# Layer 0: block transposes on VectorE from quarter loads, and the bias table split in its compact form

## The chip, the cores and the metric

The kernel runs on one core of a Trainium2 chip. Time is device time in microseconds (us) of one execution; the time of a kernel is the median of several runs. The engines are called PE (TensorE matmul), PEld (its weight loads), DVE (VectorE), ACT (ScalarE), POOL (GpSimd) and SP (SyncE, which here only issues DMAs).

## What is computed

Four layers follow each other on x of shape (4, 8, 512, 512), axes t, b, n, d: each adds to x a function of the group-normalised x. Only layer 0 is touched by the change. It is a block of spiking attention over four time steps t:

```python
def lif(x):                      # over t
    v = v + (xt - v) / 2; spk = v >= 1; v = v * (1 - spk)
q = heads(lif(bn(x @ Wq.T)));  k = heads(lif(bn(x @ Wk.T)));  v = heads(lif(bn(x @ Wv.T)))
scores = einsum('tbhnd,tbhmd->tbhnm', q, k) * scale + bias_table[rel]     # rel = m - n + N - 1
out = lif(einsum('tbhnm,tbhmd->tbhnd', scores, v))
out = out * gate_scale + gate_shift
x = x + lif(bn(out @ Wp.T))
```

There is no softmax, so q (k^T v) and (bias) v are taken apart. H is 8 heads of 64. The input of layer 0 is normalised over groups of two batch entries b for each t. Layer 1 is a 13x13 depthwise convolution, layer 2 a quantised 3x3 convolution, layer 3 a 3x3 convolution.

## The kernel before, in words

Layer 0 works in 32 steps (b, t), t innermost, the state h of each neuron kept in SBUF from one t to the next. A software pipeline handles in iteration n: attention of step n (`attend`), its output projection (`project_out`) interleaved with the input projections of step n+1 (`project_in` for v, k and q in this order, four column groups c each), and the transposes for step n+2.

- **Loads.** `load_x` (line 408) issues four DMAs of 256 KB on SP, one for each 128 rows n: the x of step n+2 (name x), the residual of step n (xr) and the x whose statistics the next group of batch entries needs (xs). All come from one pool, x0, of 10 tiles.
- **Statistics.** `count` (line 414) runs bn_stats on each tile; `group_stats` (lines 175 to 195) turns them into the mean and the reciprocal deviation of a group: small DVE operations, two PE matmuls (line 178) and a power on POOL (line 195).
- **Transposes.** The projections contract over d, so x has to have d on the partitions. `transposed` (lines 460 to 468) lets PE transpose four 128x128 blocks against an identity into a PSUM bank ps_xT (two banks), and DVE evicts it with the normalisation (line 468) to a tile xn. Four xn tiles make a step, six are in the pool. `transpose` is called for k = 0, 1 during the q projection and for k = 2, 3 after it.
- **Projections.** `project_in` (line 485) multiplies in f32 (two PE passes for each of four blocks k) into a PSUM bank ps_in of the pool ps_mm, two banks. For v and k DVE forms the potential (line 450), the spikes (line 490) and what is kept (line 457), and POOL adds a constant row (line 458). For q, which stays transposed, DVE forms potential (443, or 441 at t = 0), spikes (427) and rest (429), and ACT the half (433). At t = 3 nothing is kept.
- **Attention.** `attend` multiplies k by v (ps_kv, line 501), masks the result to kvb (DVE, line 506), and for each pair of heads j multiplies kvb by q (ps_a, line 513, one bank) and v by the bias (ps_b, line 521, two banks). The bias is a Toeplitz matrix, held as three bf16 parts, toep[0..2], each 128 x 8 x 896; DVE forms the spikes so from both (lines 533, 536, 427, 429).
- **Output.** `project_out` (line 548) multiplies so by the projection's weights in two parts into ps_mm, DVE adds spikes to the residual (559) and takes statistics of the sum (563), POOL mirrors the edges (570) and stores (575).

Before the first step the weights are prepared. `load_weights` loads a matrix with row c*128 + p on partition p. `along_free` (lines 331, 332) lays a per-column scale along the free dimension: four times a DVE product of the identity with a column, and a matmul of ones with it. `prepare_in` multiplies v's and k's weights by this scale (line 344). `prepare_bias` (lines 356 to 364) loads for each head the table as a 128x896 Hankel matrix in f32 and splits it in three parts: three ACT casts, one subtraction on DVE and one on POOL. `prepare_out` prepares the output weights.

The order of the instructions on each engine is fixed when the program is built, from their order in the code, a scheduler's own estimate of when operands are ready, and pool sizes. `issue_after(op)` keeps what is traced in its block behind op on op's engine only; it is no wait for other engines. A DMA issued on SP or ACT that waits for a buffer or a completion counter keeps all later ones of that queue waiting.

Of the kernel before, what the change touches and what calls it, by code (L numbers as in the profile page):

```python
# [30 lines left out]
F32 = mybir.dt.float32  # L34
# [9 lines left out]
T, B, N, D, H = 4, 8, 512, 512, 8  # L44
DH = D // H
NC = N // P
G = 4
PAIR = B // G
EPS = 1e-5
# [215 lines left out]
def layer0(  # L265
# [2 lines left out]
    nc = tc.nc  # L268
    half_scale = 0.5 / math.sqrt(D)

    ps_mm = s.enter_context(tc.tile_pool(name="ps_mm", bufs=2, space=PSUM))
    ps_b = s.enter_context(tc.tile_pool(name="ps_b", bufs=2, space=PSUM))
    ps_1 = s.enter_context(tc.tile_pool(name="ps_1", bufs=1, space=PSUM))
    wpool = s.enter_context(tc.tile_pool(name="w0", bufs=1))
# [16 lines left out]
    a_half = wpool.tile([P, 4, NC], F32, name="a_half")  # L291
    c_half = wpool.tile([P, 4, NC], F32, name="c_half")

    xp = s.enter_context(tc.tile_pool(name="x0", bufs=10))
    small0 = s.enter_context(tc.tile_pool(name="s0", bufs=4))
    x1p = s.enter_context(tc.tile_pool(name="x1p", bufs=2))
    state = s.enter_context(tc.tile_pool(name="state", bufs=1))
# [1 line left out]


    def load_weights(n, engine):
        engine.dma_start(wT[n], i[f"wT_{n}"].rearrange("(c p) e -> p c e", p=P))

    nc.scalar.dma_start(cols.rearrange("p a b -> p (a b)"), i["cols"])
    bn = cols[:, :16, :].rearrange("p (n s) c -> p n s c", s=4)
    ones = wpool.tile([P, P], F32, name="ones")
    nc.vector.memset(ones, 1.0)

    def batch_norms():

        neg_half = wpool.tile([P, 4, NC], F32, name="nh0")
        nc.vector.memset(neg_half, -0.5)
        nc.vector.tensor_scalar_add(a_half, bn[:, :, 3, :], EPS)
        nc.gpsimd.tensor_tensor(a_half, a_half, neg_half, op=ALU.pow)
        nc.vector.tensor_mul(a_half, a_half, bn[:, :, 0, :])
        nc.vector.tensor_scalar_mul(a_half, a_half, 0.5)
        c = c_half[:, :3, :]
        nc.vector.scalar_tensor_tensor(
            c, bn[:, :3, 2, :], -1.0, a_half[:, :3, :], op0=ALU.mult, op1=ALU.mult
        )  # L320
        nc.vector.scalar_tensor_tensor(
            c, bn[:, :3, 1, :], 0.5, c, op0=ALU.mult, op1=ALU.add
        )

    def along_free(cols):


        ps = ps_mm.tile([P, D], F32, tag="mm", name="ps_free")
        for c in range(NC):
            diag = work.tile([P, P], F32, tag="diag", name="diag", bufs=2)  # L330
            nc.vector.tensor_scalar_mul(diag, ident, cols[:, c : c + 1])
            nc.tensor.matmul(
                ps[:, c * P : (c + 1) * P], lhsT=ones, rhs=diag, start=True, stop=True
            )
        return ps

# [2 lines left out]

    def prepare_in(n):  # L340
        j = "qkvp".index(n)
        scale = along_free(a_half[:, j, :])
        for k in range(NC):
            nc.vector.tensor_mul(wT[n][:, k, :], wT[n][:, k, :], scale)  # L344
        return nc.scalar.mul(c_twice[n], along_free(c_half[:, j, :]), 2.0).ins

    def prepare_bias():


        n_u = toep[0].shape[2]  # L350
        table = i["table"]
        hankel = state.tile([P, 2, n_u], F32, tag="h_o", name="hankel")
        rest = state.tile([P, 2, n_u], F32, tag="h_p", name="rest")
        for h in range(H):
            src, r = hankel[:, h % 2, :], rest[:, h % 2, :]
            nc.scalar.dma_start(
                src, bass.AP(table.tensor, h * (2 * N - 1), [[1, P], [1, n_u]])
            )
            dst = [w[:, h, :] for w in toep]
            nc.scalar.copy(dst[0], src[:, ::-1])  # L360
            nc.vector.tensor_sub(r, src[:, ::-1], dst[0])
            nc.scalar.copy(dst[1], r)
            nc.gpsimd.tensor_sub(r, r, dst[1])
            nc.scalar.copy(dst[2], r)

    def load_out():
        wp32 = work.tile([P, NC, D], F32, tag="so", name="wp32")
# [3 lines left out]
    def prepare_out(wp32):  # L371
        gate_scale, gate_shift = cols[:, 16, :], cols[:, 17, :]

        shift = ps_1.tile([P, NC], F32, tag="misc", name="shift")
        for e in range(NC):
            for k in range(NC):
                nc.tensor.matmul(
                    shift[:, e : e + 1],
                    lhsT=wp32[:, k, e * P : (e + 1) * P],
                    rhs=gate_shift[:, k : k + 1],  # L380
                    start=k == 0,
                    stop=k == NC - 1,
                )
        c = c_half[:, 3, :]
        nc.vector.tensor_sub(c, shift, bn[:, 3, 2, :])
        nc.vector.tensor_mul(c, c, a_half[:, 3, :])
        nc.vector.scalar_tensor_tensor(c, bn[:, 3, 1, :], 0.5, c, op0=ALU.mult, op1=ALU.add)

        nc.scalar.mul(
            c_twice["p"].rearrange("p (g v) -> p g v", g=PH), phases(along_free(c)), 2.0  # L390
        )
        scale = work.tile([P, D], F32, tag="v", name="scale_p", bufs=3)
        nc.scalar.copy(scale, along_free(a_half[:, 3, :]))
        for k in range(NC):
            wp = work.tile([P, D], F32, tag="v", name="wp_k", bufs=3)
            nc.vector.scalar_tensor_tensor(
                wp.rearrange("p (g v) -> p g v", g=PH), phases(wp32[:, k, :]),
                gate_scale[:, k : k + 1], phases(scale), op0=ALU.mult, op1=ALU.mult,
            )
            nc.scalar.copy(wpT[0][:, k, :], wp)  # L400
            nc.vector.tensor_sub(wp, wp, wpT[0][:, k, :].bitcast(F32))
            nc.scalar.copy(wpT[1][:, k, :], wp)

    def load_x(b, t, name):
        got = []
        for c in range(NC):
            xt = xp.tile([P, D], F32, tag="x", name=f"{name}_{b}_{t}_{c}")
            nc.sync.dma_start(xt, x_in[t, b, c * P : (c + 1) * P, :])
            got.append(xt)
        return got  # L410

    def count(xt, stats, pair):
        for c in range(NC):
# [43 lines left out]
            nc.vector.scalar_tensor_tensor(h, v, 1.0, v, op0=ALU.is_lt, op1=ALU.mult)  # L457
            nc.gpsimd.tensor_add(h, h, c_twice[n])  # L458

    def transposed(xt, k, m, r):  # L460

        ps = ps_1.tile([P, N], F32, tag="xT", name="ps_xT", bufs=2)
        for c in range(NC):
            nc.tensor.transpose(
                ps[:, c * P : (c + 1) * P], xt[c][:, k * P : (k + 1) * P], ident
            )
        xk = work.tile([P, N], F32, tag="xn", name="xn", bufs=6)
        nc.vector.tensor_scalar(xk, ps, m, r, op0=ALU.subtract, op1=ALU.mult)
        return xk

    def new_spikes():
# [126 lines left out]
    def transpose(n, k):  # L598
        if n <= last:
            b, t = steps[n]  # L600
            xns.setdefault(n, []).append(transposed(xs[n], k, *norms[b // PAIR, t]))
            if k == NC - 1:
                del xs[n]

    def load(n):
        if n <= last:
            xs[n] = load_x(*steps[n], "x")

    def next_group(n):
        g, j = divmod(n + 1, PAIR * T)  # L610
# [12 lines left out]
        return band, eye, x, bt  # L623

    load(0)
    load_weights("v", nc.sync)
    statistics(0, 0, 0, xs[0])
    statistics(0, 0, 1, load_x(1, 0, "xs"))
    batch_norms()
    for k in range(NC):  # L630
        transpose(0, k)
    with tc.issue_after(prepare_in("v")):
# [4 lines left out]
    for n in range(-1, last + 1):  # L637
# [7 lines left out]
        if n + 1 <= last:  # L645
            spikes = new_spikes()
            g, j = divmod(n + 1, PAIR * T)
            if n >= 0:
                load(n + 2)
            if j == 2 and g > 0:  # L650
                norm1(g - 1, ps_1)
            if g == 0 and n >= 0 and n + 2 < T:
                statistics(0, n + 2, 0, xs[n + 2])
                statistics(0, n + 2, 1, load_x(1, n + 2, "xs"))
            if n >= 0:
                next_group(n)
        for a, name in enumerate("vkq"):
            for c in range(NC):
                if n + 1 <= last:
                    did = project_in(name, c, xns[n + 1], spikes, steps[n + 1][1])  # L660
                if (n, name, c) == (-1, "v", 0):
                    first += [prepare_in("k"), did, potentials[0]]
                    with ExitStack() as behind:
                        for op in first:
                            behind.enter_context(tc.issue_after(op))
                        load(1)
                        statistics(0, 1, 0, xs[1])
                        statistics(0, 1, 1, load_x(1, 1, "xs"))
                if n >= 0 and a < 2 and c % 2:
                    project_out(so, 2 * a + c // 2, residual[2 * a + c // 2], b, t)  # L670
                if a == 2 and c % 2:
                    transpose(n + 2, c // 2)
# [4 lines left out]
        if n < 0:  # L677
            with ExitStack() as behind:
                for op in first:
                    behind.enter_context(tc.issue_after(op))  # L680
                prepare_bias()
                prepare_out(load_out())
                next_group(n)
                bands1(tc, i, band1d, w_sum, eye, ps_mm, state)
            for name in "op":
                h_of[name] = state.tile([P, NC, N], F32, tag=f"h_{name}", name=f"h_{name}")
# [593 lines left out]
```

## Time and profile before

| what | value |
|---|---|
| median of 3 runs | 2997.45 us (2994.02 to 2998.33) |
| profiled execution, its time | 2993.4 us |
| its span from first to last instruction | 2991.6 us |
| mean granted PE clock | 0.988 |
| PE busy | 2900.4 us (97%) |
| DVE busy | 2243.8 us (75%) |
| POOL, ACT busy | 1035.6 us (35%), 550.0 us (18%) |
| first matmul of the v projection (line 485) | 21.05 us |
| ps_kv of step 0, 1, 31 | 88.59, 166.39, 2089.56 us |
| DMA in a settled step | 67 to 68 GB/s, 22% of the queues' time |

The page cuts the span into 40 slices of 75 us and gives each engine's busy share in tenths. Matmuls are pipelined, so the duration of one (592 ns for a projection pass) is longer than the distance between two (430 ns); a PE that shows as busy can still lose a little between groups. Layer 0 takes the first 28 slices. A window's busy time is that of all its instructions on an engine, overlaps counted once.

### The profile page before, as it was taken

Reading aid. Unit: us, or ns where it says so; the run is one execution under the profiler, and the core shown is the slowest. Engines: PE = TensorE matmul, PEld = TensorE weight load, DVE = VectorE, ACT = ScalarE, POOL = GpSimd, SP = SyncE. Lnnn points to the kernel's source line nnn. Section 1 sums busy time; section 2 is a strip of 40 time slices with the busy share of each in tenths; the row PEclk is TensorE's granted clock in tenths of the full one; section 3 lists DMA queues with packets and bytes.
Section 4 is the critical chain, followed back from the end, with each engine's and each line's share of the span. In section 5 each row is a group of like instructions: output and inputs, shape, how many; then the busy total and the mean of one; then the engine's idle time right before and its main releaser. Section 6 shows DMA issues by size and latency. Waiting matters only on the chain. (4 is left out here: it accounts for less than half of the span.)

```text
span 2991.6 us, 37579 instructions
## 1 busy us (share of the span) xinstructions
PE 2900.4 (97%) x13343; PEld 1391.5 (47%) x13377; DVE 2243.8 (75%) x3883; ACT 550.0 (18%) x859; POOL 1035.6 (35%) x1928
## 2 busy tenths in 40 slices
PE   7999999999999999999999999999999999689999
PEld 3545555555555555555555555555333333223334
DVE  7887788788769868967986886786665566888880
ACT  2200010011010001001000100100111121676674
POOL 3332233333224333323432333341211112676650
PEclk9999999999999999999999999999999999889999
DMA  5312222222222221212221111111877778698865
GB/s 189 109 58 65 78 65 65 65 64 65 78 65 65 65 72 58 78 65 65 65 69 47 58 43 51 51 56 45 208 203 216 204 210 227 160 198 223 220 175 147
DMA packets 274651, 322.16 MB, mean 108 GB/s; under 512 B 21495, under 2 KB 171711, under 8 KB 274351
## 3 DMA queue, kind: packets, MB, share of 16 engines
q1 hardware_dynamic: 212304, 236.70, 29.3%
q0 software_dynamic: 20192, 56.83, 6.1%
q10 hardware_dynamic: 41967, 26.23, 3.0%
q8 instruction: 105, 1.72, 0.3%
q14 instruction: 83, 0.68, 0.1%
HBM read 210.57 MB, written 103.60 MB: 105 GB/s over the span
## 5 line engine op out<-in xcount | busy, mean ns | idle before, releaser
L485 PE MATMUL ps_in<-w_v,xn 128*128 128x512 f32 x1024 | 465.0, 603 | 2.6 <-DVE w_kq L344 2.6
L485 PE MATMUL ps_in<-xn,w_kq 128*128 128x512 f32 x1024 | 452.9, 595 | 5.1 <-DVE v_q L441 3.7
L485 PE MATMUL ps_in<-w_kq,xn 128*128 128x512 f32 x1024 | 449.8, 592 | 0.7 <-DVE v_k L450 0.7
L797 PE MATMUL ps_conv<-x,bt 112*64 112x512 f32 x2048 | 445.1, 592 | 0.1
L521 PE MATMUL ps_b<-toep,vtok 128*64 128x512 bf16 x3072 | 373.6, 383 | 0.0
L433 ACT ACTIVATE h_q<-v_q,c_half 128x512 f32<-128x512 f32 x96 | 69.3, 722 | 1550.6 <-DVE v_q L429 1164.1
L570 POOL COPY x1s<-x1s 128x2 f32<-128x2 f32 (+1 forms) x1024 | 227.4, 276 | 297.8 <-DVE x1s L559 297.8
L548 PE MATMUL ps_out<-wp,so 128*128 128x512 f32 x1024 | 308.5, 443 | 0.0
L458 POOL TENSOR_TENSOR h_v<-h_v,c_v 128x512 f32<-128x512 f32 x96 | 123.2, 1283 | 517.1 <-DVE h_v L457 505.4
L485 PEld LDWEIGHTS ps_in<-xn,w_kq 128*128 128x128 f32 x1024 | 191.9, 190 | 228.1 <-issue 212.4
L485 PEld LDWEIGHTS ps_in<-w_kq,xn 128*128 128x128 f32 x1024 | 194.2, 190 | 222.0 <-issue 205.2
L485 PEld LDWEIGHTS ps_in<-w_v,xn 128*128 128x128 f32 x1024 | 191.6, 192 | 216.9 <-issue 211.5
L797 PEld LDWEIGHTS ps_conv<-x,bt 112*64 112x64 f32 x2048 | 146.1, 135 | 288.4 <-issue 286.7
L521 PEld LDWEIGHTS <-vtok 128*64 128x64 bf16 x3072 | 207.6, 111 | 126.2 <-issue 4.9
L1182 PE MATMUL ps_conv<-x,band_t 64*64 64x512 f32 x2040 | 246.4, 599 | 3.1 <-DVE band_t L1151 3.1
L1047 POOL COPY u<-x 128x512 f32<-128x512 f32 (+1 forms) x172 | 208.7, 1247 | 95.8 <-issue 48.5
L548 PEld LDWEIGHTS ps_out<-wp,so 128*128 128x128 f32 x1024 | 192.5, 188 | 94.6 <-issue 57.8
L559 DVE SCALAR_TENSOR_TENSOR x1s<-v_p,xr 128x256 f32<-128x256 f32 x256 | 187.0, 770 | 14.9 <-DMA x<-x1s 3.9
L195 POOL TENSOR_TENSOR grstd_x<-grstd_x,neg_half 128x1 f32<-128x1 f32 (+1 forms) x28 | 20.9, 748 | 474.0 <-DVE grstd_x L194 474.0
L815 POOL DMA_DIRECT2D x<-xo x128 | 71.4, 565 | 312.5 <-ACT xo L804 298.2
L804 ACT ACTIVATE xo<-ps_conv,off 128x512 f32<-128x512 f32 x128 | 87.7, 687 | 430.6 <-PE ps_conv L797 316.0
L458 POOL TENSOR_TENSOR h_k<-h_k,c_k 128x512 f32<-128x512 f32 x96 | 122.8, 1279 | 116.4 <-DVE h_k L457 116.4
(191 smaller groups left out, 3557.8 us busy)
## 6 DMA issues: line engine op xcount, KB each, us to landing
x<-x SPq DMA_DIRECT2D x64, 917.0 KB
x<-x SPq DMA_DIRECT2D x168, 256.0 KB
x<-x1s POOLq DMA_DIRECT2D x128, 262.0 KB, 2.5
x<-in_x SPq DMA_DIRECT2D x128, 256.0 KB
xr<-in_x SPq DMA_DIRECT2D x128, 256.0 KB
out<-o SPq DMA_DIRECT2D x164, 192.0 KB
xs<-in_x SPq DMA_DIRECT2D x112, 256.0 KB
x<-xo ACTq DMA_DIRECT2D x128, 128.0 KB
```

The costliest lines, as they stand in the source:

```text
L433: nc.scalar.activation(h, v, AF.Identity, bias=c_col, scale=0.5)
L458: nc.gpsimd.tensor_add(h, h, c_twice[n])
L485: mm = nc.tensor.matmul(ps, lhsT=lhsT, rhs=rhs, start=k == 0, stop=k == NC - 1)
L521: nc.tensor.matmul(pb[two * DH : (two + 1) * DH, :], lhsT=v[:, c, h * DH : (h + 1) * DH], rhs=toep[z][:, h, u : u + N], start=c == 0 and z ...
L548: nc.tensor.matmul(ps, lhsT=so[:, k, c * P : (c + 1) * P], rhs=wpT[z][:, k, :], start=k == 0 and z == 0, stop=k == NC - 1 and z == 1,)
L559: nc.vector.scalar_tensor_tensor(own, v.rearrange("p (g v) -> p g v", g=PH)[:, two, :], 1.0, by_phase[:, two, :], op0=ALU.is_ge, op1=ALU.add,)
L570: nc.gpsimd.tensor_copy(x1[:, f, u : u + n], x1[:, fm, um - n + 1 : um + 1][:, ::-1])
L797: mm = nc.tensor.matmul(ps[q * M1 : (q + 1) * M1, :], lhsT=bt[:, z, :], rhs=xt[:, w0 : w0 + N_PS1, z : z + NV], start=z == 0, stop=z == SH ...
L804: nc.scalar.activation(xo[:, a, :], ps, AF.Identity, bias=off[:, t : t + 1])
L815: engine.dma_start(bass.AP(dst.tensor, dst.offset + (q * n_half * W1_OUT * B + b) * D + f * NV, [[B * D, W1_OUT], [W1_OUT * B * D, n_half] ...
L1047: nc.gpsimd.tensor_copy(u[:n_p, j, :].rearrange("p (v g) -> p v g", g=PH), x[:, j, :].rearrange("p (g v) -> p v g", g=PH),)
L1182: mm = nc.tensor.matmul(ps[j][b * HALF : (b + 1) * HALF, :], lhsT=band[half, b, dx, :], rhs=x3[half, s0 + j, dx : dx + D], start=dx == 0, ...
```

## The change

It replaces PE's transposes in layer 0 by DVE's. A DVE transpose exchanges rows and columns within each 32x32 block only; so x is loaded in four quarters, each on 32 partitions: partition 32 q + s holds, for the rows n = 32 j + s, the 128 columns from 128 q on, in runs of 512 bytes. One DVE transpose of 128 x 512 then gives xn for k: partition 32 q + a holds column 128 q + 32 k + a. The weights' rows are loaded in the same order. The normalisation runs in place on the loaded tile, before the transposes. The quarter tile (128 x 2048) has a pool of its own with one buffer; the pool x0 shrinks to 6 tiles; ps_mm takes the two freed PSUM banks.

The bias table is split while compact, on 24 partitions of 341 entries; the three bf16 parts are stored to DRAM in 16 copies of each head and loaded from there as Toeplitz tiles, 24 loads of 16 partitions each on ACT's queue. The scales are transposed to rows once, and `along_free` selects a row by a matmul with a column of the identity, broadcast, as weights. At the start, v's weights follow the statistics' tiles on SP.

```diff
-    ps_mm = s.enter_context(tc.tile_pool(name="ps_mm", bufs=2, space=PSUM))
+    ps_mm = s.enter_context(tc.tile_pool(name="ps_mm", bufs=4, space=PSUM))
...
-    xp = s.enter_context(tc.tile_pool(name="x0", bufs=10))
+    xp = s.enter_context(tc.tile_pool(name="x0", bufs=6))
+    xqp = s.enter_context(tc.tile_pool(name="xq0", bufs=1))
...
     def load_weights(n, engine):
-        engine.dma_start(wT[n], i[f"wT_{n}"].rearrange("(c p) e -> p c e", p=P))
+        rows = i[f"wT_{n}"].rearrange("(q c a) e -> q a c e", c=NC, a=SQ)
+        for q in range(P // SQ):
+            engine.dma_start(wT[n][q * SQ : (q + 1) * SQ], rows[q])
...
+    def as_rows_of(cols):
+        n = cols.shape[1]
+        ps = ps_mm.tile([n, P], F32, tag="mm", name="ps_rows")
+        nc.tensor.transpose(ps, cols, ident)
+        rows = wpool.tile([4 * NC, P], F32, tag="rows", name="rows", bufs=2)
+        nc.scalar.copy(rows[:n], ps)
+        return rows[:n]
...
         for c in range(NC):
-            diag = work.tile([P, P], F32, tag="diag", name="diag", bufs=2)
-            nc.vector.tensor_scalar_mul(diag, ident, cols[:, c : c + 1])
+            at = NC * j + c
             nc.tensor.matmul(
-                ps[:, c * P : (c + 1) * P], lhsT=ones, rhs=diag, start=True, stop=True
+                ps[:, c * P : (c + 1) * P], lhsT=ident[:n, at : at + 1].to_broadcast([n, P]),
+                rhs=rows, start=True, stop=True,
             )
...
+    def split_bias():
+        n_c = 3
+        n_e = n_h // n_c
+        parts = tc.dram_tile([3, H, n_copy, n_h], BF16, name="bias_parts")
+        src = state.tile([H * n_c, n_e], F32, tag="h_o", name="bias_table")
+        nc.scalar.dma_start(src, bass.AP(i["table"].tensor, 0, [[n_e, H * n_c], [1, n_e]]))
+        part = state.tile([H * n_c, 3, n_e], BF16, tag="h_p", name="bias_part")
+        for z in range(3):
+            dst = part[:, z, ::-1]
+            nc.vector.tensor_copy(dst, src)
+            if z < 2:
+                nc.vector.tensor_sub(src, src, dst)
+        for z in range(3):
+            for c in range(n_c):
+                at = (n_c - 1 - c) * n_e
+                nc.sync.dma_start(
+                    parts[z, :, :, at : at + n_e],
+                    part[c::n_c, z, :].unsqueeze(1).to_broadcast([H, n_copy, n_e]),
+                )
+        return parts
...
+        for z in range(3):
+            for m in range(P // n_copy):
+                nc.scalar.dma_start(
+                    toep[z][m * n_copy : (m + 1) * n_copy],
+                    bass.AP(
+                        parts.tensor,
+                        parts.offset + z * H * n_copy * n_h + P - 1 - m * n_copy,
+                        [[n_h - 1, n_copy], [n_copy * n_h, H], [1, toep[0].shape[2]]],
+                    ),
+                )
...
+    def load_quarters(b, t):
+        xt = xqp.tile([P, N // SQ, P], F32, tag="xq", name=f"xq_{b}_{t}")
+        rows = x_in[t, b].rearrange("(j s) (q f) -> q s j f", s=SQ, f=P)
+        for q in range(P // SQ):
+            nc.sync.dma_start(xt[q * SQ : (q + 1) * SQ], rows[q])
+        return xt
...
-    def transposed(xt, k, m, r):
-        ps = ps_1.tile([P, N], F32, tag="xT", name="ps_xT", bufs=2)
-        for c in range(NC):
-            nc.tensor.transpose(
-                ps[:, c * P : (c + 1) * P], xt[c][:, k * P : (k + 1) * P], ident
-            )
+    def transposed(xt, k):
         xk = work.tile([P, N], F32, tag="xn", name="xn", bufs=6)
-        nc.vector.tensor_scalar(xk, ps, m, r, op0=ALU.subtract, op1=ALU.mult)
+        nc.vector.transpose(
+            xk.rearrange("p (j s) -> p j s", s=SQ), xt[:, :, k * SQ : (k + 1) * SQ]
+        )
         return xk
...
-            xns.setdefault(n, []).append(transposed(xs[n], k, *norms[b // PAIR, t]))
+            if k == 0:
+                m, r = norms[b // PAIR, t]
+                flat = xs[n].rearrange("p j f -> p (j f)")
+                nc.vector.tensor_scalar(flat, flat, m, r, op0=ALU.subtract, op1=ALU.mult)
+            xns.setdefault(n, []).append(transposed(xs[n], k))
...
     load(0)
-    load_weights("v", nc.sync)
-    statistics(0, 0, 0, xs[0])
-    statistics(0, 0, 1, load_x(1, 0, "xs"))
-    batch_norms()
+    normed = batch_norms()
+    a_rows = as_rows_of(a_half.rearrange("p n c -> p (n c)"))
+    c_rows = as_rows_of(c_half[:, :3, :].rearrange("p n c -> p (n c)"))
+    with tc.issue_after(normed):
+        statistics(0, 0, 0, as_rows(xs[0]))
+        statistics(0, 0, 1, load_x(1, 0, "xs"))
+        load_weights("v", nc.sync)
+        bias_parts = split_bias()
```

In the output weights' preparation the scale is now taken before the constant row, and the constant is turned into a row first.

## The prediction, made before the changed kernel ran

> **What bounds the kernel now.** I read the page's busy shares first, then the windows of single steps, then the timelines of TensorE (PE) and VectorE (DVE), and last the groups that touch the transposes. Layer 0 ends at about 2110 us of the 2991.6 us span, so two thirds of the time is at stake.
>
> ```profile
> PE   7999999999999999999999999999999999689999
> ...
> DVE  7887788788769868967986886786665566888880
> ```
>
> PE is full from the second slice to the end of layer 0, and DVE is the second busiest. Only the first slice has a hole. The windows below run from one step's k-by-v matmuls (kv, line 501) to the next step's; columns are the length, then busy time (count) of PE, weight loads, DVE, ScalarE (ACT), GpSimd (POOL), the granted clock, DMA share, GB/s.
>
> ```profile
> 300.70:363.89 63.19, 63.17 (x266) 33.98 (x264) 44.25 (x77) 2.16 (x3) 17.89 (x44) 1.00 0.22 68
> 363.89:428.07 64.18, 63.98 (x270) 34.19 (x268) 55.64 (x89) 7.57 (x12) 25.70 (x49) 1.00 0.22 67
> 428.07:491.64 63.57, 63.47 (x266) 33.72 (x264) 56.85 (x86) 5.41 (x8) 25.13 (x48) 1.00 0.22 68
> 491.64:556.10 64.46, 64.17 (x270) 34.05 (x268) 47.13 (x82) 3.24 (x5) 15.51 (x41) 1.00 0.22 67
> ...
> 21.05:166.39 145.34, 132.77 (x472) 66.72 (x472) 124.66 (x213) 36.55 (x49) 55.67 (x67) 0.93 0.41 133
> 166.39:235.09 68.70, 65.46 (x260) 33.22 (x259) 57.72 (x91) 6.13 (x9) 25.70 (x49) 0.95 0.12 41
> ```
>
> A settled step takes 63.2 to 64.5 us and PE fills it. DVE is at 69 to 89 percent: two steps of four are light (about 45 us), two heavy (56 to 57 us). From kv at 300.70 to the last kv at 2089.56 there are 28 steps, 63.9 us each. What leaves PE's path there shortens the step, as long as DVE keeps up.
>
> **Transposes off PE.** The groups by tile, then PE's timeline (start, length):
>
> ```profile
> L464 PE MATMUL ps_xT<-ident,x x512: 272/273/477, 3.8 to 2028.5; 128*128 128x128 f32 x171
> L468 DVE TENSOR_SCALAR xn<-ps_xT,gmean_x,grstd_x x128: 797/802/811, 19.2 to 2029.7; 128x512 f32<-128x512 f32 x128
> ```
>
> ```profile
> 299.83 1.04 PE L464 MATMUL ps_xT<-ident,x 128*128 128x128 f32 x8
> 300.70 0.83 PE L501 MATMUL ps_kv<-vtok,k 128*128 128x128 bf16 x12
> 301.56 0.66 PE L464 MATMUL ps_xT<-ident,x 128*128 128x128 f32 x4
> 302.05 0.39 PE L501 MATMUL ps_kv<-vtok,k 128*128 128x128 bf16 x4
> 302.37 1.91 PE L521 MATMUL ps_b<-toep,vtok 128*64 128x512 bf16 x15
> ```
>
> The 273 ns is a latency; the pitch counts. Eight transposes hold PE from 299.83 to 300.70 (0.87 us), four from 301.56 to 302.05 (0.49 us), four more at 292.53 to 292.96 (0.43 us). Sixteen a step: 1.79 us. Over 28 steps that is 50 us.
>
> **What DVE gets instead.** It loses four PSUM evictions a step, 4 x 0.80 = 3.2 us. It gains four block transposes of 128x512 and one in-place normalise of 128x2048. No row shows a transpose. Nearest are single-source or two-source SBUF operations of 128x512 f32[...], 0.68 to 0.69 us (lines 429, 457); the low end is the 0.42 us of a tensor_scalar[...] (line 427), the high end twice 0.69. I take 0.69: 2.8 us. For the normalise the same 0.42 us row gives the fast price[...]. I take 1.2. DVE's sum is +0.8 us a step (ends: -0.3 and +4.7), so a heavy step holds about 57.5 us of DVE in 62.
>
> [...] The trace has PE at 107 to 112 ns in the stream, so PE is the cheaper engine[...]. [...] here the cheap engine is the full one.
>
> **A new wait.** In the program's order after the change, q's last group is followed on PE by kv (16 matmuls, 0.98 us) and only 8 or 9 of ps_b (1.0 us) before the first ps_a, which needs q's spikes and kvb from DVE. So the cover is 2.0 us; before it was 4.1 us (302.37 + 1.56 less 299.83), partly made of the transposes. Queued behind the waiting ps_a are all other ps_b of the step, though they need nothing from DVE. What DVE does then, before:
>
> ```profile
> 427.48 0.75 DVE L443 SCALAR_TENSOR_TENSOR v_q<-ps_in,a_half,h_q 128x512 f32<-128x512 f32 x1 [1.57 <-PE ps_in L485]
> 428.15 0.80 DVE L468 TENSOR_SCALAR xn<-ps_xT,gmean_x,grstd_x 128x512 f32<-128x512 f32 x1
> 428.87 0.42 DVE L427 TENSOR_SCALAR q<-v_q 128x512 f16<-128x512 f32 x1
> 429.20 0.80 DVE L468 TENSOR_SCALAR xn<-ps_xT,gmean_x,grstd_x 128x512 f32<-128x512 f32 x1
> 429.92 0.68 DVE L429 SCALAR_TENSOR_TENSOR v_q<-v_q 128x512 f32<-128x512 f32 x1
> 430.52 0.80 DVE L468 TENSOR_SCALAR xn<-ps_xT,gmean_x,grstd_x 128x512 f32<-128x512 f32 x1
> 431.24 0.68 DVE L506 TENSOR_TENSOR kvb<-ps_kv,c 128x512 f16<-128x512 f32 x1
> ```
>
> PE finished q at 427.20 and kvb ended 4.7 us later, with three evictions in the way. After the change v_q, q and kvb follow each other: 0.28 + 0.75 + 0.42 + 0.68 = 2.1 us. A DVE that is on time makes PE wait about 0.3 us. In heavy steps it is late: before, q's first v_q began at 417.81 where its matmuls ended at 416.5, and the changed order puts the four statistics of the next group (0.6 us pitch each) into the k and q stages, and two transposes between q's third and fourth group. DVE regains 1.8 us on each q group (1.66 of work against 3.44 on PE). Added up, its fourth v_q starts about 1.3 us late: a wait of some 1.3 us. Between bounds of 0 and 2.5 us I take 1.3. The four PSUM banks of ps_mm (two before) let PE run ahead until there and save perhaps 0.2 us a step of present waits. Net: 1.79 - 0.8 (mean of 0.3 and 1.3) + 0.2 = 1.2 us a step for 21 steps, 1.6 for the last 7, which load no statistics: 36 us.
>
> **Edits at no cost while their cover lasts.** The quarter load has one buffer: it is issued on SP once the last transpose of the step before has read it, about at q's end, and is first needed by the normalise, which stands after the third head pair of attention, 11 us later. Four issues (0.4 us each), some 2 us of latency, and 1 MB in 512-byte packets: layer 1's 524-byte packets reach 338 to 370 GB/s, so 3 us. That is 6.6 us, 4 us in hand. Behind it on SP are two residual tiles and four statistics tiles, needed 20 us later. If the cover is gone, DVE stalls for the excess and the rest of attention's spikes with it. The normalise falls in attention, where POOL has no work between 420.2 and 447.2; [...] which beside POOL's adds would cost what line 490 shows (1.99 us instead of 0.43), and here nothing.
>
> **The start.** Gone: 24 ACT casts (0.93 us), 8 DVE and 8 POOL subtractions (1.1 and 1.9 us), the scaled-identity products. New: five DVE operations on 24 partitions (about 0.5 us each) ahead of the first statistics, nine stores on SP ahead of step 1's loads, 24 loads of 229 KB on ACT's queue; 17 of them stand behind q's ACT work and land near 80 us (3.9 MB at the 390 GB/s of the first loads). w_v is now issued after the statistics' tiles. The first matmul waits for statistics, normalise and a transpose in a row: about 23.6 us instead of 21.05. Then PE runs v, k and q nearly undisturbed, to 67 us instead of 80. But step 1's and 2's statistics now follow q on DVE, step 2's quarters wait for step 1's transposes, and PE's in-order queue holds their small matmuls ahead of most of attention: 24 statistics instructions at 0.6 us (15 us), two normalises and six transposes (6.5), the load (7) and three chains to a group's factors at 3 us put attention's rest near 105 us. Weight preparation after that leaves kv of step 1 at about 168 instead of 166.4 (156 to 178). The 68.7 us step behind it (3.2 us wait at ps_a, 0.95 clock) should take 64, the next 63.5 instead of 65.6. Net gain 5 us, from -8 to +15.
>
> **Sum.** 36 + 5 = 41 us off the profiled execution's 2993.4 us: 2952. It lies 4 us under the median of the runs, 2997.45, so I forecast 2956.
>
> **Rivals.** (a) No new wait: DVE stays in time, the 1.79 us arrive whole, 50 + 10 at the start: 2937. For it: 4 to 6 us of DVE idle per heavy step; against it: the idle lies in the v stage, not before ps_a. (b) DVE paces the heavy steps or the start loses 10 to 15 us: steady gain 0.7 us a step (20), start -5: 2982, down to 2970. For it: 89 percent DVE; against: light steps recover. (c) Slower: block transposes run at two or more cycles an element. Two stand between q's third group and kvb, so each 0.7 us extra on both adds 1.4 us of wait; at 1.4 us a transpose the gain of a step is gone, at 2.1 us each step loses 1.2 us or more: 28 x 1.2 = 34, so 3030. No row excludes it[...]. (d) The edit yields nothing because another engine paces PE throughout: 2997.
>
> **Chances.** Forecast case 0.48, (a) 0.25, (b) 0.19, (c) 0.05, (d) 0.03. The range of 2926 to 2980 takes in the forecast case, most of (a) with a better start, and most of (b). About 0.2% (6 us) is what a measurement tells from no change: faster 0.92, same 0.04, slower 0.04.
>
> **What would show it.** No ps_xT on PE; steps of 62 to 62.8 us; a wait of ps_a for kvb of 0.3 us in light and 1 to 2 us in heavy steps; transposes near 0.69 us and the normalise near 1.2 us; kv of step 1 near 168 us; no DVE wait for the quarters after the start. I am wrong if transposes take over 1 us, if DVE waits for the quarters in each step, or if kv of step 1 comes outside 156 to 178 us.

## The result, and the profile after

| | before | after |
|---|---|---|
| median | 2997.11 us (2994.02 to 2998.33, 4 runs) | 2961.28 us (2960.19 to 2965.81, 4 runs) |
| profiled execution, its span | 2993.4, 2991.6 us | 2960.48, 2958.7 us |
| ps_kv of steps 0, 1, 3, 31 | 88.59, 166.39, 300.70, 2089.56 us | 89.15, 195.90, 322.34, 2051.31 us |

The ratio is 0.9885 (95% interval 0.9868 to 0.9902): 36 us faster, where 41 were forecast. The total came out near the forecast; its parts did not. The rows of PE, DVE and the granted clock on the page, in slices of 74 us:

```profile
PE   7499999999999999999999999999999999689999
DVE  5488688778778868877976887886656556887870
PEclk9599999999999999999999999999999999889999
```

The hole of the first slice has grown into the second, where PE is busy 4 tenths and its clock is half. From the third slice on PE is full, as it was. Windows from one ps_kv to the next, columns as in the windows of before:

```profile
89.15:195.90 106.75, 74.62 (x275) 38.02 (x275) 70.12 (x123) 12.37 (x22) 26.39 (x50) 0.79 0.47 99
195.90:257.78 61.88, 61.77 (x253) 31.24 (x252) 56.28 (x98) 4.29 (x7) 25.75 (x49) 1.00 0.32 85
...
322.34:383.64 61.30, 61.27 (x250) 30.86 (x249) 45.00 (x78) 1.51 (x3) 17.96 (x44) 1.00 0.26 70
383.64:445.52 61.88, 61.88 (x253) 31.41 (x252) 53.10 (x88) 8.12 (x13) 25.69 (x49) 1.00 0.26 69
445.52:506.90 61.38, 61.27 (x250) 30.86 (x249) 54.45 (x88) 5.12 (x9) 25.16 (x48) 1.00 0.27 70
```

Each settled step is some 2 us shorter than its counterpart, and PE is idle for at most 0.11 us in those shown. The step from 89.15 us takes 106.75 us where it took 77.8, with 32 us of PE idle and a clock of 0.79. Three terms make up the profiled difference of 32.9 us:

- **Settled steps**, kv 3 to kv 31: 1728.97 us against 1788.86, 61.75 a step against 63.89. Gain 59.9 us.
- **Start**, up to kv 3: 21.6 us later. Step 1's kv is 29.5 us later; steps 1 to 2 and 2 to 3 give back 6.8 and 1.1 us.
- **After kv 31**: 907.4 against 902.0 us, 5.4 us longer.

The last term fits no edit: over the kernels below that stretch takes 901.5 to 907.4 us without pattern (the version of the float32 loads has 902.0, the same with idle transposes added 906.5). The kv times are free of it.

What DVE does now, by the groups of the tile xq (count, then shortest, median and longest in ns, then first and last start), and all that PE waits for from 322 to 2060 us:

```profile
L508 DVE STREAM_TRANSPOSE xn<-xq x128: 668/702/712, 19.5 to 1989.0; 128x512 f32<-128x512 f32 x128
L646 DVE TENSOR_SCALAR xq<-xq,gmean_x,grstd_x x32: 1336/1340/1912, 18.1 to 1941.9; 128x2048 f32<-128x2048 f32 x32
```

```profile
PE ps_a L555 <- DVE kvb L548: 5.4, 6, 1.8
```

The transposes cost what was forecast (0.69), the normalise a little more (1.34, where the author's estimate was 1.2). But ps_a waits only 6 times for kvb in 28 steps, 0.2 us a step on average, where 0.3 to 1.3 us were forecast for every step.

In heavy steps DVE has not more but less to do: they held 55.64 and 56.85 us of it and hold 53.10 and 54.45. The spikes of k and q got cheaper by more than the new operations add. Here are two heavy steps, before (363.89 to 491.64 us) and after (383.64 to 506.90 us), with busy us and mean ns:

```profile
L490 DVE TENSOR_SCALAR k<-v_k 128x512 bf16<-128x512 f32 x8 | 12.1, 1507 | 0.3
L427 DVE TENSOR_SCALAR q<-v_q 128x512 f16<-128x512 f32 x8 | 6.4, 796 | 0.1
```

```profile
L532 DVE TENSOR_SCALAR k<-v_k 128x512 bf16<-128x512 f32 x8 | 8.2, 1023 | 0.1
L472 DVE TENSOR_SCALAR q<-v_q 128x512 f16<-128x512 f32 x8 | 3.9, 483 | 0.2
```

That is 3.2 us a step. In eight steps of the kernel before, from 300 us on, such an operation takes 0.43 us alone and 1.0 to 2.0 us while one of POOL's additions (line 458) runs. In the new order they meet for a shorter time: a k beside an addition takes 1.2 us on average instead of 1.5, a q 0.6 instead of 1.8.

**The start.** ACT's timeline (start, length; ACTq rows are DMA issues, in brackets what ended the idle time before) and SP's:

```profile
72.28 52.18 ACTq L390 DMA_DIRECT2D toep<-bias_parts  x17
124.56 0.59 ACT L422 COPY scale_p<-ps_free 128x512 f32<-128x512 f32 x1 [51.63 <-DMA toep<-bias_parts]
```

```profile
17.45 24.80 SPq L379 DMA_DIRECT2D bias_parts<-bias_part  x9
43.38 3.59 SPq L450 DMA_DIRECT2D xq<-in_x  x4
48.23 27.87 SPq L441 DMA_DIRECT2D xs<-in_x  x8
```

ACT's queue needs 52 us to issue the last 17 bias loads, and the output weights' scale waits behind them until 124.56 us. PE's order has the small matmuls of that preparation ahead of most of attention: ps_a resumes at 139.56 us and the first ps_out comes at 153.73 us (121.00 before). On SP the nine bias stores take 24.8 us, with step 1's loads behind them. And the queues hold each other up; from SP's waits between 0 and 126 us (in total, times, longest):

```profile
SPq L441 <- DMA toep<-bias_parts: 23.5, 2, 14.1
...
SPq L379 <- DMA toep<-bias_parts: 10.8, 1, 10.8
```

The built program shows why: SP's and ACT's DMAs take turns on eight completion counters, and each waits for an earlier one on its counter, whichever queue that is on. A bias load waits for a load of x, which waits for DVE to free its buffer, and the other way round: no bias load is issued between 84.2 and 97.8 us, while SP waits 10.7 us for DVE, until 91.53 us, to load the next quarters. So the stores' 24.8 us are mostly waiting too: 10.8 us of the ninth store for the first bias load, and 7.6 us for loads of k's and q's weights.

**Theories.** A: the start is lost to the bias table's new path (narrow loads, stores, queues). B: it is lost to the statistics, which now stand behind q on DVE and PE and have one quarter buffer. For the settled steps: PE's transposes are the whole gain, or the two added banks have a part, and DVE has room, or has just enough.

### The profile page after: what moved, and what is told of

Its sections match the earlier page's. It is cut to its first block, busy times and chain, and to the rows that moved or that the text cites. A ratio compares the mean times of both kernels' runs of the same rounds, so it can differ in the third digit from the quotient of the medians.

```text
span 2958.7 us, 36595 instructions
## 1 busy us (share of the span) xinstructions
PE 2836.9 (96%) x12868; PEld 1309.2 (44%) x12868; DVE 2194.5 (74%) x3887; ACT 530.1 (18%) x838; POOL 1017.7 (34%) x1920
## 5 line engine op out<-in xcount | busy, mean ns | idle before, releaser
L527 PE MATMUL ps_in<-w_v,xn 128*128 128x512 f32 x1024 | 458.9, 599 | 7.1 <-DVE w_v L358 7.1
L527 PE MATMUL ps_in<-xn,w_kq 128*128 128x512 f32 x1024 | 444.6, 592 | 0.0
L563 PE MATMUL ps_b<-toep,vtok 128*64 128x512 bf16 x3072 | 365.6, 382 | 3.4 <-DMA bands<-in_w 3.4
L1232 PE MATMUL ps_conv<-x,band_t 64*64 64x512 f32 x2040 | 252.8, 612 | 3.1 <-DVE band_t L1201 3.1
L563 PEld LDWEIGHTS <-vtok 128*64 128x64 bf16 x3072 | 175.1, 110 | 157.0 <-issue 7.4
L1137 DVE SCALAR_TENSOR_TENSOR x<-ps_conv,inv,u 128x512 f32<-128x512 f32 (+1 forms) x172 | 121.8, 745 | 58.2 <-PE ps_conv L1130 29.9
```

The costliest lines, as they stand in the source:

```text
L527: mm = nc.tensor.matmul(ps, lhsT=lhsT, rhs=rhs, start=k == 0, stop=k == NC - 1)
L563: nc.tensor.matmul(pb[two * DH : (two + 1) * DH, :], lhsT=v[:, c, h * DH : (h + 1) * DH], rhs=toep[z][:, h, u : u + N], start=c == 0 and z ...
L1137: done["DVE"] = nc.vector.scalar_tensor_tensor(own, ps[:n_p, :], w["inv"][:n_p], u[:n_p, j, :], op0=ALU.mult, op1=ALU.add, accum_out=sums[ ...
L1232: mm = nc.tensor.matmul(ps[j][b * HALF : (b + 1) * HALF, :], lhsT=band[half, b, dx, :], rhs=x3[half, s0 + j, dx : dx + D], start=dx == 0, ...
```

## Experiments: which part did what

All medians are of 4 runs (5 in one case), beside runs of the kernel before on the same chip (2990 to 2995 us); "kv n" is the start of step n's ps_kv.

**The bias part undone.** The body of `prepare_bias` of before in place of `split_bias` and the loads:

```diff
-        bias_parts = split_bias()
...
-                prepare_bias(bias_parts)
+                prepare_bias()
```

> The changed kernel with the earlier bias preparation put back (8 float32 loads of 128 partitions, three copies on ACT, one subtraction on DVE and one on POOL a head); the transposes on DVE, the quarter loads and the rest stay. Theory A (what the start lost is the bias path: 9 stores on SP's queue for 24.8 us ahead of xq_1, and 24 loads of 16 partitions that held ACT's queue from 72.3 to 124.5 us): the statistics row goes to PE at about 105 instead of 125 us, attention resumes by 115 instead of 133.7, the k/v projection of step 1 starts at 166 to 175 instead of 195.9 us, and the median is 2930 to 2942. Theory B (it is the statistics chain itself, which now stands behind q on DVE and PE, with one quarter's buffer): the projection of step 1 still starts at 188 to 200 us and the median is 2955 to 2966; if the 8 subtractions get in DVE's way there, up to 2972.

Measured: 2922.36 us, ratio 0.9763 (0.9749 to 0.9778); kv 1 at 163.25, kv 3 at 290.98 us; settled steps 61.70 us. Theory A holds and B falls as the main cause: with the statistics where the change puts them, the start is 9.7 us earlier than before.

**The bias part alone**, on the kernel before: `split_bias` and the 24 loads, all else as before.

> The kernel before with the compact bias split alone (9 stores and 24 loads of 16 partitions in place of 8 loads of 128 and the work on ACT, DVE and POOL); transposes on PE, whole loads of x. Theory A: the queues of SP and ACT are held as in the changed kernel, the projection of step 1 starts at 180 to 196 us instead of 166.4, and the median is 3010 to 3027. Theory B: the bias path is hidden here too, step 1's projection stays at 160 to 170 us and the median at 2990 to 3001 (below 2997 if what ACT and DVE are spared was late there).

Measured: 3032.53 us, ratio 1.0125 (1.0108 to 1.0142); kv 1 at 209.41 us, settled steps 63.89 us. Worse than theory A's numbers, since here PE waits for the parts themselves:

```profile
PE ps_b L540 <- DMA toep<-bias_parts: 44.4, 3, 23.9
```

So the parts add up: the transposes with all that goes with them are worth -71 us, the compact bias +39 us, with either form of the other. Measured up to kv 3, without the stretch after kv 31, the compact bias costs 31 us in the changed kernel and 38 us in the one before.

**Two banks for the projections** (`ps_mm`, bufs=4 to 2).

> The changed kernel with two PSUM banks for the projections (ps_mm) instead of four; two banks stay empty. A settled step of the changed kernel is 2.14 us shorter than before, and the transposes that left PE are 1.79 of that. If the other 0.35 us is the banks' doing: settled steps of 62.1 us instead of 61.75 and a median near 2971. If the banks do nothing there (PE gains it elsewhere, as in order): 2959 to 2963. If the projections' evictions on DVE are late behind the transposes without the two banks: 0.5 us or more a step, 2977 or above.

Measured: 2963.48 us (2960.15 to 2964.37); 61.87 us a step. The banks are worth 0.13 us a step at most.

**Sixteen transposes put back on PE**, in the kernel with the old bias preparation:

```diff
+        ps = ps_1.tile([P, N], F32, tag="xT", name="ps_xT", bufs=2)
+        for c in range(NC):
+            nc.tensor.transpose(ps[:, c * P : (c + 1) * P], ident, ident)
```

They transpose the identity, and nobody reads the result.

> The kernel with DVE's transposes and the earlier bias preparation (2922 us), to which 16 transposes a step on PE are added again, of the identity into two PSUM banks that nobody reads (ps_mm back at two banks). If PE's time is the whole gain of a step: a settled step goes from 61.70 to 63.5 us (16 x 0.11 = 1.79), and the median to 2972 to 2981. If the step of 63.89 of the kernel before comes back: 2983 to 2990, so that banks and transposes account for all of 2.14. If PE has room elsewhere: below 2960.

Measured: 2960.24 us (2959.49 to 2964.64), which tests nothing as a total: since they wait for nothing, the order of the program pulled over half of them into the start's idle time on PE, and steps 3 to 13 have none. From kv 22 to kv 28 each step has its 16, and there the comparison is clean: 63.22 us a step, against 61.54 without them, 61.69 with two banks and none, and 63.70 before. PE's timeline there:

```profile
1669.19 0.60 PE L494 MATMUL ps_xT<-ident 128*128 128x128 f32 x4
1669.63 7.03 PE L511 MATMUL ps_in<-xn,w_kq 128*128 128x512 f32 x16
1676.50 1.47 PE L494 MATMUL ps_xT<-ident 128*128 128x128 f32 x12
```

The transposes are worth 1.5 to 1.7 us a step, a little less than 16 x 0.11. Most of the last 0.5 us lies in attention: from ps_kv to the first v matmul one step takes 13.65 us before (of which four transposes between ps_kv and ps_b are 0.5), 12.68 after and 12.54 here, where all sixteen stand ahead of ps_kv. In the step from 1643.78 us of the kernel before, those four start some 0.2 us late by PE's pitch, when DVE has evicted an earlier ps_xT. And the second ps_a, with only six ps_b between it and the first, starts some 0.3 us late, just after ACT has read the first out of the one bank (1648.84 us); in the step after the change fourteen ps_b stand there, and no gap shows. That is one step; no run tests this order alone.

**Each DVE transpose twice** (the same output written again).

> The changed kernel with each of DVE's 128 transposes of layer 0 done twice (the same output written again): 4 x 0.70 = 2.8 us more of DVE in each step, which has 7 to 16 us of DVE free of 61.8. If DVE's work is covered, as the 0.1 us of waiting for kvb in a settled step says: 2961 to 2968. By the forecast's rule (0.7 us more on each of the two transposes between q's third group and kvb ends in 1.4 us of waiting): 28 x 1.3 = 36 us more, near 2997. If each transpose lies on the path: 28 x 2.8 = 78 us more, near 3040.

Measured: 2980.28 us (2974.28 to 2983.36), kv 3 at 330.21 us, 62.28 us a step. By the profiled spans it is 23 us slower than the changed kernel: 8 in the start, 15 in the settled steps, 0.54 us a step for 2.8 us of DVE work. PE's waits from 331 to 2075 us:

```profile
PE ps_a L556 <- DVE kvb L549: 15.4, 12, 3.5
```

DVE's room is real but nearly used up: the forecast's wait of ps_a for kvb appears here, 0.55 us a step instead of 0.2, with 2.8 us more of DVE work in each.

## Experiments: what makes the bias path slow

**Loads from POOL's queue** (`nc.scalar.dma_start` to `nc.gpsimd.dma_start` in `prepare_bias`).

> The changed kernel with the 24 loads of the bias parts issued from POOL's queue instead of ACT's; nothing else moves. Two readings of how the compact form costs its 39 us. Blocking: the loads hold up what is queued behind them on ACT (scale_p at 124.6 us); then scale_p runs by 100 us, attention resumes by 115, step 1's k/v projection starts at 165 to 176, median 2922 to 2938. Traffic: the loads themselves are slow (24 loads, 5.5 MB, 52 us[...]), so that whoever issues them, the bias products wait for the parts; then the wait of ps_b for the parts appears (20 us or more), step 1's projection stays at 185 to 200, median 2950 to 2965. If POOL's own work is held up (its adds for h_v and h_k), the first k/v projection moves from 89 to 100 or later, and the median is above 2965.

Measured: 2957.92 us (2956.40 to 2959.91); scale_p at 73.27 us, but kv 1 at 195.22. Freeing ACT's queue alone gains nothing. Nor does the wait of ps_b appear: the first projection of step 1 waits 16.4 us for its x instead, because the statistics wait for xs loads (11.2 us for one) that now compete with the bias; before that, SP stood 27.6 us waiting for a load on ACT's queue (bands), on the shared counters. Neither reading was right as put; traffic and counters delay other loads.

**8 copies, and 32** (`n_copy` 16 to 8 or 32): 48 loads of 8 partitions, or 12 of 32. Bytes and pieces of the loads stay.

> The changed kernel with 8 shifted copies of each bias part in place of 16: the stores on SP carry half (0.39 MB), and the parts are loaded by 48 DMAs of 8 partitions instead of 24 of 16; bytes and pieces of the loads stay. If the few partitions of a load set its pace, the loads take twice as long (100 us instead of 52), and the median is 2995 to 3015. If pieces and bytes set it, the loads take as long as before, the stores some 12 us less on SP: median 2945 to 2962.

> The changed kernel with 32 shifted copies of each bias part: 12 loads of 32 partitions, stores of 1.57 MB. If the few partitions of a load set its pace, the loads take some 26 us instead of 52, against stores of some 50 us on SP that hold up xq_1 and xs by 25 us: median 2955 to 2975. If pieces and bytes set it, the loads stay at 50 us and the stores come on top: median 2975 to 2995.

Measured: 3006.16 us (2993.09 to 3011.49) with 8, PE waiting 96 us for the parts; 2943.60 us (2941.93 to 2944.78) with 32, though the stores on SP then take 28 us and carry twice the bytes. The width of a load sets its pace. Stretches in which bias loads have the DMA engines to themselves, or nearly (the last two columns are the DMA share and GB/s), all from ACT's queue: 8 partitions, 16 (the changed kernel), 32, and the 128-partition version below, which begins among loads of x that are as wide:

```profile
112.00:140.00 28.00, 0.62 (x4) 0.21 (x4) 0.00 (x0) 0.00 (x0) 0.00 (x0) 0.50 0.52 64
```

```profile
38.00:43.00 5.00, 5.00 (x13) 2.23 (x12) 2.08 (x4) 0.00 (x0) 2.12 (x2) 1.00 1.06 131
```

```profile
37.50:42.00 4.50, 4.50 (x12) 2.08 (x11) 1.71 (x3) 0.00 (x0) 2.33 (x2) 1.00 1.06 203
```

```profile
35.00:47.00 12.00, 12.00 (x30) 5.30 (x29) 8.99 (x17) 0.00 (x0) 2.53 (x2) 1.00 1.06 382
```

64, 131, 203 and 382 GB/s (16 partitions in another stretch, 85.5 to 88 us, 123). At 16 partitions the DMA engines show as fully busy while they move a third of what they move at 128; only at 8 partitions does the share itself drop, to 0.52, so that there fewer busy engines may be the reason as well. A full DMA share, then, does not say at what rate the engines move bytes.

**16 partitions, 8 apart.** The same loads, each spread over the tile:

```diff
-                    toep[z][m * n_copy : (m + 1) * n_copy],
+                    toep[z][m :: P // n_copy],
...
-                        parts.offset + z * H * n_copy * n_h + P - 1 - m * n_copy,
-                        [[n_h - 1, n_copy], [n_copy * n_h, H], [1, toep[0].shape[2]]],
+                        parts.offset + z * H * n_copy * n_h + P - 1 - m,
+                        [[n_h - P // n_copy, n_copy], [n_copy * n_h, H], [1, toep[0].shape[2]]],
```

> The changed kernel with the same 24 loads of 16 partitions, the same bytes and pieces, but each load's partitions 8 apart (0, 8, 16 ... 120 and so on) instead of next to each other; the copies are read with the shift that goes with it. In the changed kernel such loads reach 123 GB/s, loads of 8 neighbouring partitions 64, loads of 128 partitions 382. If it is the number of partitions (or of pieces side by side) that sets the rate: 123 GB/s as before, 52 us, median 2957 to 2965. If [...]: about twice the rate, 200 to 250 GB/s where the loads run alone, and a median of 2925 to 2945.

Measured: 2949.97 us (2949.10 to 2956.13), ratio 0.9860 (0.9843 to 0.9876). Where they are alone, in short stretches, they reach 202 GB/s and more (240 and 241 from 106.5 and 120 us) instead of 123 to 131:

```profile
84.50:86.00 1.50, 1.50 (x9) 1.50 (x9) 0.00 (x0) 0.00 (x0) 0.00 (x0) 0.50 1.00 202
```

That is the rate of 32 neighbours (203), with half as many partitions. So the number of partitions alone does not set the rate: where they lie counts as well. Why it does, no run here shows. But the time fell by 11 us only, and kv 3 by 5.3 us. The 17 loads behind q still take 47.7 us: between them the DMA engines stand idle (from 87 to 92 us for one), since each load waits its turn behind loads of x, and SP waits 10.7 us for DVE, until 91.30 us, before the next of those.

**The narrow loads asked for earlier**, ahead of step 1's x:

```diff
+                        prepare_bias(bias_parts)
                         load(1)
...
-                prepare_bias(bias_parts)
                 prepare_out(load_out())
```

> The changed kernel with its 24 narrow loads asked for ahead of step 1's loads of x, so that ACT's order holds all 24 before the four h_q of the first step, as in the version with 24 loads over all partitions (2914 us); width, bytes and pieces stay. In the changed kernel 17 of them stand behind h_q and alternate with SP's loads of step 2, which wait for DVE. If that place is the whole cost: the loads take 24 x 1.86 = 45 us from 33 us on, scale_p runs by 88 us, step 1's k/v projection starts at 155 to 163 us, median 2913 to 2923. If the narrow loads cost by their rate as well: they end past 85 us, h_q and the loads of step 1's x wait for them, step 1's projection starts at 168 to 185 us, and the median is 2928 to 2945. If place means nothing: 2957 to 2965.

Measured: 2957.80 us (2954.04 to 2961.67), kv 1 at 194.72 us. All 24 now stand ahead of h_q, and it helps nothing:

```profile
33.64 86.19 ACTq L390 DMA_DIRECT2D toep<-bias_parts  x24
119.88 1.95 ACT L478 ACTIVATE h_q<-v_q,c_half 128x512 f32<-128x512 f32 x3 [87.00 <-DMA toep<-bias_parts]
```

86 us for loads that would take 45 alone at 123 GB/s, an estimate; in the rest they wait for loads of x, which wait for DVE's statistics (SP: 18.8 us in 9 waits). The place of the loads is not the cause.

## Experiments: a version that beats both

**One copy, wide loads, PE reads backwards.** The shifted copies exist only because the Toeplitz tile runs against the table. Loaded in the table's own direction, all 128 partitions come with a step of one element, and the reversal can be left to the matmul's operand:

```diff
-    n_h, n_copy = 2 * N - 1, 16
+    n_h, n_copy = 2 * N - 1, 1
...
-            dst = part[:, z, ::-1]
+            dst = part[:, z, :]
...
-                at = (n_c - 1 - c) * n_e
+                at = c * n_e
...
+            nc.scalar.dma_start(
+                toep[z],
+                bass.AP(
+                    parts.tensor,
+                    parts.offset + z * H * n_h,
+                    [[1, P], [n_h, H], [1, toep[0].shape[2]]],
+                ),
+            )
...
-                u = P * (NC - 1 - c)
+                u, n_u = P * (NC - 1 - c), toep[0].shape[2]
...
-                            rhs=toep[z][:, h, u : u + N],
+                            rhs=toep[z][:, h, n_u - N - u : n_u - u][:, ::-1],
```

> The changed kernel with the split bias stored once (one copy, 48 KB, not reversed), loaded by 3 DMAs over all 128 partitions with the table's rows overlapping, and the reversal done by PE, which reads the bias in the bias products (96 a step) from its last element to its first. If the width of the loads is the cause: 5.5 MB at the 385 GB/s that the 128-partition loads of x reach are some 15 us instead of 52, scale_p is no longer held up, step 1's k/v projection starts at 155 to 170 us, and the median is 2905 to 2930 (the version with 128-partition float32 loads gave 2922, with ACT, DVE and POOL at work on the bias). If the start's loss sat elsewhere in the compact form (the pieces of 1792 bytes, the detour through DRAM): 2945 to 2960. If PE reads backwards more slowly, the bias products of 0.107 us grow and each step with them: at twice the time 10 us a step, above 3200.

Measured: **2910.16 us** (2907.51 to 2915.00), ratio 0.9731 (0.9715 to 0.9748); kv 1 at 147.45, kv 3 at 275.20 us. This is the fastest of the kernels: 51 us below the changed kernel and 12 below the version with the old preparation, which keeps ACT, DVE and POOL at work on the bias. Its bias loads in ACT's timeline, and the bias products by groups (busy us, mean ns); the same group of the changed kernel after it:

```profile
33.66 5.98 ACTq L389 DMA_DIRECT2D toep<-bias_parts  x3
```

```profile
L562 PE MATMUL ps_b<-toep,vtok 128*64 128x512 bf16 x3072 | 364.6, 381 | 0.0
```

```profile
L563 PE MATMUL ps_b<-toep,vtok 128*64 128x512 bf16 x3072 | 365.6, 382 | 3.4 <-DMA bands<-in_w 3.4
```

PE reads backwards at no cost (381 ns against 382).

**The same with 24 loads**, one for each head and part, over 128 partitions:

> The version that stores the split bias once and lets PE read it backwards (2910 us, 3 loads of 1.8 MB over 128 partitions), with 24 loads instead of 3, one a head and part: as many DMAs, bytes and pieces of 1792 bytes as the changed kernel, but over all 128 partitions. In the program SP's and ACT's DMAs take turns on eight completion semaphores, and each waits for the one eight places ahead of it, on either queue. If the rate of narrow loads was the cost: each takes 0.6 us, step 1's k/v projection starts at 147 to 153 us, median 2907 to 2915. If it was the number of DMAs and their waiting for one another: the loads stretch over 30 us or more, ACT's work behind them is held up, and the median is 2930 to 2960.

Measured: 2914.42 us (2911.63 to 2915.25), kv 1 at 152.15 us.

```profile
34.18 21.23 ACTq L390 DMA_DIRECT2D toep<-bias_parts  x24
```

Same number of loads, same bytes and pieces, and the same place ahead of h_q as the 24 narrow ones that took 86 us and gave 2957.80. By the medians the number of loads costs some 4 us (the runs of the two versions overlap); what costs the rest is narrowness, with the stores of 16 copies (24.3 us on SP, 10.5 with one copy), which this pair does not separate from it. But of those 24.3 us, 10.3 are a wait for a narrow load. And 8 copies had stores as short, 10.3 us, and were the slowest, while 32 copies had the longest, 28.1 us, and were faster than 16; so the stores are not the main part.

## Why the prediction was right in sum and wrong in parts

The sum was 36 + 5 = 41 us; the profiled executions give 60 - 22 - 5 = 33. Two steps failed with opposite signs; that the total still came out near the forecast is luck.

- **Transposes off PE, 1.79 us a step: right.** Putting them back cost 1.5 to 1.7 us.
- **DVE's prices: right, its sum wrong.** The new operations take 0.70 and 1.34 us, against 0.69, read off other operations on DVE, and 1.2, an estimate that no trace of before showed; but instead of 0.8 us more a heavy step holds some 2.5 us less of DVE: 53 to 54.5 us, not 57.5. The sum put the spikes of k and q at no change, and they lost 3.2 us a step.
- **"A new wait", 0.8 us a step on average: wrong.** It is 0.2 us. By the forecast's own rates (1.8 us regained on each of three q groups, two transposes of 0.69 in between) a fourth v_q that is 1.3 us late needs a lag of some 5 us at the first, an estimate. In the heavy step that ends at 445.52 us the first v_q (437.99 us) comes only 2.8 us after its matmuls. DVE does the work up to the fourth in 7.6 us, to 445.6, while PE needs 10.3 for three groups, and the fourth starts at 445.80, when PE has just finished. So the lag was put too high; the cheaper spikes fit that, but no run tests the link. Rival (a), no new wait, was the right one for the steps, and even its 50 us are 10 short. The doubled transposes show that the mechanism was sound and only its size off: the steps grow by 0.54 us when each gets 2.8 us more of DVE work.
- **Four banks, 0.2 us: nearly nothing**, at most 0.13 us.
- **Quarter load hidden: right.** DVE waits for it once, 5.7 us up to 99 us in the start.
- **"The start", net gain of 5 us, kv of step 1 at 168: wrong**, 195.90 and a loss of 21.6 us. The term that failed is the 24 bias loads, put at the rate of the first loads, 390 GB/s (3.9 MB in 10 us, landing near 80). They ran to 124.5 us: loads of 16 neighbouring partitions moved 123 to 131 GB/s where they were alone, and they stood in turn with loads that wait for DVE. At the 123 GB/s measured the 3.9 MB take 32 us instead of 10, an estimate. The nine stores were named and not priced: 24.8 us on SP, 18.4 of them waiting. With the old bias preparation the rest of that step holds: kv 1 at 163.25 us against 168, a net gain of 9.7 us against 5. Rival (b) had the start's loss as 10 to 15 us in all but named another cause.
- **Statistics behind q: right in kind.** Their small matmuls hold PE by 30 us from 20 to 200 us (6 waits of up to 9.5 us), but with the old bias preparation this shrinks to 3.3 us.
- **PE the cheaper engine, but the full one (97% busy): right.** It transposes four blocks of 128x128 in 0.43 us, against 0.70 on DVE, and still the transposes on DVE, with all that goes with them, gain 71 us.

What stays open: how the 39 us of the bias path divide between the loads' rate, their taking turns with SP's loads, and the stores; a higher rate alone gained 5 us up to kv 3 and 11 in total, another place or another queue nothing up to kv 3 (322.60 and 325.19 us against 322.34) and 3 us each in total, the one-copy version with wide loads 51. And the 0.5 us a step in attention.

## What to carry to other kernels

Price a DMA by what it writes to, not by the best rate in the profile: a load onto 16 neighbouring partitions ran at a third of the widest loads' rate here (131 against 382 GB/s), with the DMA share at its full value (1.06). A form that is compact in memory is not compact in traffic: here it moved 5.5 MB in 1792-byte pieces where the old one moved 3.7 MB; look for a layout that loads wide and let the consumer's access pattern do the reversal. When a forecast's total comes true, check its terms: two errors of 24 and 27 us cancelled here, and mending the second gained 51 us, more than the change itself.

## What the runs showed of the hardware that was not expected

- A load's rate by the partitions that it writes: 8 neighbours 64 GB/s at a DMA share of 0.52, 16 neighbours 131 at 1.06, 32 neighbours 203 at 1.06, 16 partitions 8 apart 202 at 1.00, all 128 382 at 1.06.
- A bf16 operand of 512 columns read backwards costs PE nothing: 381 ns against 382.
- The 32 shift matmuls took 6.99 us from 81.90 us, at a granted clock of 0.50; before the change they took 3.56 us from 80.85 us, at 1.00.
- The spikes of k and q on DVE take 0.43 us, but 1.0 to 2.0 us beside an addition on POOL (the kernel before, eight steps).
